# First diffusion step: column-scaled rows as a GpSimd product in place of their own transposes

## The chip, the cores and the metric

The kernel runs on one core of a Trainium2 chip. The metric is the time of one execution in microseconds on the device, the median of repeated runs. Engines are named as the profile names them: PE (TensorE matmul), PEld (its weight load), DVE (VectorE), ACT (ScalarE), POOL (GpSimd), SP (SyncE, which only issues DMAs). A name with q behind it (SPq, POOLq) is the engine's queue.

## What is computed

There are N = 2708 rows of D = 512 numbers. A graph attention layer comes first (layer 0). Then comes layer 1, a diffusion with three branches and two steps, here cut to what matters:

```
S  = adj + eye(N)
Rf = S / S.sum(axis=1)[:, None]      # each row divided by its row sum
Rb = S / S.sum(axis=0)[:, None]      # each row divided by the column sum of the same index
Xf = Xb = Xa = X
for s in range(2):
    A  = softmax of the nucleus (mass 0.9) of each row of the logits made from Xa
    Xf, Xb, Xa = Rf @ Xf, Rb @ Xb, A @ Xa
    Z += Xf @ U1[s] + Xb @ U2[s] + Xa @ U3[s]
out = x + layernorm(X + Z) * gamma + beta
```

In the first step `Xf` and `Xb` both start from X, so both are S @ X, with row i divided by a row sum in one and by a column sum in the other.

## The kernel before

The 2708 rows are 22 tiles of up to 128 rows (`NT`), handled in 11 pairs (`pairs`) and in 6 quads of two pairs (`quads`). Layer 0 runs to about 1095 us of the span, the first diffusion step to about 2300 us, and the second to the end. Inside a step the order on PE, ACT, DVE and SP is the order of the Python code (a manual schedule); POOL's order and that of layer 0 are left to a scheduler.

For each pair a step does the following.

- `Logits.products` (L521 on PE, L523 on ACT) makes the pair's logits `p`, `Logits.exp` looks at them on ACT (L553, L560), and `search` finds each row's nucleus on DVE: a few rounds of masses (L629), then `finish` (L806, L808, L730), then `branch`, which reads a flag into a DVE register and takes an arm of a switch (L890). `p` has four buffers, so the products of pair g + 2 wait until the search of pair g is through its branch.
- `attended` transposes the kept weights on PE (L1016, copied by ACT at L1020) and multiplies them with the values `va` (L1035). ACT takes the result out of PSUM with its scale (L1043) and POOL stores it as `xa_d` (L1045). The PSUM tiles `a` have two buffers.
- `part` makes S @ X for a quad. `product` (L967) runs between the other matmuls, half of the 22 row blocks in an even pair and half in the next, odd one. Then `scaled` runs for each of the quad's tiles and each of the two scales: ACT scales out of PSUM into `xe` (L977, `rinv` or `cinv`), POOL stores that as `xfb_d` (L978), and `split_rows` splits it into two halves for the second step: two DVE instructions (L181, L182) and one store by POOL (L183, to `fhl_d` or `bhl_d`). The split has two buffers. So the odd pairs 1, 3, 5, 7 and 9 hold the splits, eight in a full quad; in DVE's queue they lie between the rounds and `finish` of the next pair's search.
- `diffused` loads the pair's rows of `xfb_d` back (L1001 on SP), both branches. `turned_rows` transposes them (L147 on PE, four 128x128 transposes a tile) and ACT copies the result out of PSUM into `v_t` (L149).
- `mixed` adds up the three products with U1, U2 and U3 in one PSUM tile per row tile (L1076), with the weight rows `u_k` loaded by SP (L1074). Before the matmuls of one branch are issued, the rows of the next branch are turned. The order is U1, U2, U3. In the last pair of the first step (`final`) it is U3, U1, U2. `project` (L160, L165 to L173) makes keys and queries for the second step, stored to `kq_d`.

Between layer 0 and the first step the sums are inverted: `rinv`, `cinv`, and `ratio`, which is the row sum over the column sum. The first step begins with four loads of `keys` (L930) and loads of the queries `q_t` (L509) on SP.

Of the kernel before, what the change touches and what calls it, by code (L numbers as in the profile page):

```python
# [9 lines left out]
F32 = mybir.dt.float32  # L10
# [5 lines left out]
OP = mybir.AluOpType  # L16
AX = mybir.AxisListType
PSUM = bass.MemoryType.PSUM
# [6 lines left out]
P = 128  # L25
# [28 lines left out]
def kernel(  # L54
# [19 lines left out]
    nc = tc.nc  # L74
# [5 lines left out]
    KD = D // P  # L80
    NT = -(-N // P)
    rows = [min(P, N - i * P) for i in range(NT)]
    cols = [slice(i * P, i * P + rows[i]) for i in range(NT)]
# [7 lines left out]
    G = 2  # L91
# [3 lines left out]
    dram = ctx.enter_context(tc.tile_pool(name="dram", bufs=1, space=DRAM))  # L95
# [17 lines left out]
    xfb_d = dram.tile([2, N, D], F32, name="xfb_d")  # L113
    xa_d = dram.tile([N, D], F32, name="xa_d")
    en_d = dram.tile([H, N], F32, name="en_d")
    rank_d = dram.tile([NT * P], BF16, name="rank_d")

    ident = const.tile([P, P], F32, name="ident")
# [6 lines left out]
    rinv = const.tile([P, NT], F32, name="rinv")  # L125
    cinv = const.tile([P, NT], F32, name="cinv")
    ratio = const.tile([P, NT], F32, name="ratio")

    def row_bcast(ap, n):
        return bass.AP(tensor=ap.tensor, offset=ap.offset, ap=[[0, P], [1, n]])  # L130
# [71 lines left out]
    with ExitStack() as l0:  # L202
# [13 lines left out]
        with tc.tile_pool(name="l0w", bufs=1) as wp, tc.tile_pool(name="l0p", bufs=2) as pp, \  # L216
# [13 lines left out]
            for k in range(KD):  # L230
                nc.sync.dma_start(
                    out=w_sb[:, k, :].rearrange("p (h d) -> p h d", h=H),
                    in_=w_gat[:, k * P:(k + 1) * P, :].rearrange("h p d -> p h d"),
# [27 lines left out]
            for t in range(NT):  # L261
                pr = rows[t]
                h = hts[t]
                pt = ps.tile([P, KD, P], F32, name="tp")
# [50 lines left out]
        small = l0.enter_context(tc.tile_pool(name="l0small", bufs=3))  # L315
# [82 lines left out]
        for ci, tiles in enumerate(tchunks):  # L398
# [4 lines left out]
            for t in range(NT):  # L403
                pr = rows[t]
# [16 lines left out]
            for grp, r_b in zip(hgroups, r_bs):  # L421
                po = [ps_o.tile([P, 512], F32, name="po")[:DV] for _ in grp]
                for t in range(NT):
                    pr = rows[t]
# [11 lines left out]
            final = ci == len(tchunks) - 1  # L436
# [17 lines left out]
    for r, c0, c1 in [(P, 0, NFULL), (rows[-1], NFULL, NT)]:  # L454
        if c0 == c1:
            continue
        s = (slice(0, r), slice(c0, c1))
        for v, inv in ((rsum, rinv), (csum, cinv)):
            nc.vector.tensor_scalar(v[s], v[s], 1.0, 1e-12, op0=OP.add, op1=OP.max)
            nc.vector.reciprocal(inv[s], v[s])  # L460
        nc.vector.tensor_mul(ratio[s], cinv[s], rsum[s])

# [449 lines left out]
    for s in range(STEPS):  # L914
        last = s == STEPS - 1
        with ExitStack() as st:
# [3 lines left out]
            up = st.enter_context(tc.tile_pool(name=f"s{s}u", bufs=4, reuse_waits="tile"))  # L920
            parts = None if last else st.enter_context(tc.tile_pool(name=f"s{s}parts", bufs=2, reuse_waits="tile"))
            small = st.enter_context(tc.tile_pool(name=f"s{s}small", bufs=2, reuse_waits="tile"))
# [20 lines left out]
            def part(half, b):  # L943

                if b // 2 >= len(quads):
                    return []
                quad = quads[b // 2]  # L950
                first = b % 2 == 0
                w = len(quad) * P
                hl_d = (fhl_d if first else bhl_d) if last else vhl_d
                cs = range(NT) if last else range(0, NT // 2) if first else range(NT // 2, NT)
                steps = []

                def product(c):
                    if c == 0:
                        half[:] = [ps_s.tile([P, D], F32, name=f"q{i}") for i in range(len(quad))]
                    hl = sp.tile([P, 2, D], F32R, name="hl", bufs=3)  # L960
                    nc.sync.dma_start(out=hl.bitcast(F32), in_=hl_d[c * P:(c + 1) * P])
                    s_r = sp.tile([P, 2 * G * P], F32R, name="s_r")
                    nc.sync.dma_start(out=s_r[:, :w].bitcast(F32),
                                      in_=s_d[c * P:(c + 1) * P, quad[0] * P:quad[0] * P + w])
                    for j in range(len(quad)):
                        for h in range(2):
                            nc.tensor.matmul(half[j], lhsT=s_r[:, j * P:(j + 1) * P], rhs=hl[:, h],  # L967
                                             start=(c == 0 and h == 0), stop=(c == NT - 1 and h == 1))

                def scaled(t, ps, i, inv, to):  # L970
                    pr = rows[t]

                    if last and b < 2 and t % 2:
                        x = work.tile([P, D], F32, name="xw", bufs=2)
                    else:
                        x = work.tile([P, D], F32, name="xe", bufs=2 if last else 4)
                    nc.scalar.activation(x[:pr], ps[:pr], AF.Copy, scale=inv[:pr, t:t + 1])  # L977
                    nc.gpsimd.dma_start(out=xfb_d[i, cols[t], :], in_=x[:pr])  # L978
                    if not last:
                        split_rows(parts, nc.vector, x[:pr], t, to)  # L980

                steps += [lambda c=c: product(c) for c in cs]
                if last or not first:
                    for j, t in enumerate(quad):
                        if first or not last:
                            steps.append(lambda j=j, t=t: scaled(t, half[j], 0, rinv, fhl_d))
                        if not first:
                            steps.append(lambda j=j, t=t: scaled(t, half[j], 1, cinv, bhl_d))
                return steps

            def paced(steps, n):
                for step in steps[:n]:
                    step()
                del steps[:n]

            def diffused(grp):
                out_ = []
                for i in range(2):
                    for t in grp:
                        x = work.tile([P, D], F32, name=f"x{i}")  # L1000
                        nc.sync.dma_start(out=x[:rows[t]], in_=xfb_d[i, cols[t], :])  # L1001
                        out_.append(x)
                return out_[:len(grp)], out_[len(grp):]

            def attended(grp, keep, rden, fills, others, then):

# [50 lines left out]
            def turned_rows(grp, v):  # L1057
                return [transposed(up, ps_t, v[i], rows[t], "v_t") for i, t in enumerate(grp)]

            def mixed(grp, v_t, xf, xb, xa, others, fills, final=False):  # L1060

                pz = [ps_a.tile([P, D], F32, name="a") for _ in grp]
                if final:

                    v_t = turned_rows(grp, xa)
                    for i, t in enumerate(grp):
                        project(small, ps_t.tile([P, 512], F32, name="t"), v_t[i], t, s + 1)
                for n, u in enumerate((u3, u1, u2) if final else (u1, u2, u3)):  # L1070
                    nxt = turned_rows(grp, ((xf, xb) if final else (xb, xa))[n]) if n < 2 else None
                    for k in range(KD):
                        u_k = up.tile([P, D], F32, name="u_k", bufs=4 if last else 3)
                        nc.sync.dma_start(out=u_k, in_=u[s, k * P:(k + 1) * P, :])  # L1074
                        for i, t in enumerate(grp):
                            nc.tensor.matmul(pz[i][:rows[t]], lhsT=v_t[i][:, k, :rows[t]], rhs=u_k,  # L1076
                                             start=(n == 0 and k == 0), stop=(n == 2 and k == KD - 1))
                        paced(others, 1)
                        if n < 2 and k < 3:
                            paced(fills, 1)  # L1080
                    if n == 2 and not last and not final:
                        for i, t in enumerate(grp):
                            project(small, ps_t.tile([P, 512], F32, name="t"), v_t[i], t, s + 1)
                    v_t = nxt
                out_ = []
                for i, t in enumerate(grp):
                    pr = rows[t]
                    y = work.tile([P, D], F32, name="yo")
                    nc.scalar.copy(y[:pr], pz[i][:pr])
                    z = work.tile([P, D], F32, name="xw", bufs=2) if last else va[:, t, :]  # L1090
                    if last:
                        nc.sync.dma_start(out=z[:pr], in_=y_d[cols[t], :])
                    nc.gpsimd.tensor_tensor(y[:pr], y[:pr], z[:pr], op=OP.add)  # L1093
                    if not last:
                        nc.gpsimd.dma_start(out=y_d[cols[t], :], in_=y[:pr])
                    out_.append((t, y))
                return out_
# [66 lines left out]
            with tc.manual_schedule(engines={PE, ACT, DVE, SP}):  # L1164
# [18 lines left out]
                for g in range(-1, NP):  # L1183
# [18 lines left out]
                    if g >= 0:  # L1202
                        others.insert(0 if g else len(others) // 3, lambda g=g: rows_in.extend(diffused(pairs[g])))
                        final = g == NP - 1 and not last
# [72 lines left out]
```

## Time and profile before

| | us |
|---|---|
| runs (three), median | 3711.15 |
| lowest and highest | 3710.86, 3714.24 |
| the profiled execution's own time | 3711.47 |
| its span in the profile | 3709.7 |
| mean granted TensorE clock | 0.963 |
| layer 0, until the first product of logits | 1095.3 |

The profile is of one execution. Its span runs from the first to the last instruction on the engines, so the execution's own time is 1.8 us longer. "Busy" is the time that an engine's instructions took. A view of waits says which engine's line waited for which line, with the total, the number of times and the longest. A timeline's rows have start, length, engine, line, operation, operands (out<-in, partitions x elements), the count of merged instructions, and in brackets the idle time before them with what ended it. One matmul of the source is two records on PE where it is done in two passes, as at L1076 and L1035.

### The profile page before, as it was taken

To read this page: it belongs to the slowest core of one execution; us is meant where nothing else is said; L and a number is where in the kernel's file an instruction comes from. 1 tells how busy PE (TensorE), PEld (TensorE's weight loads), DVE (VectorE), ACT (ScalarE), POOL (GpSimd) and SP (SyncE) were. 2 spreads that over 40 slices of the span, in tenths; PEclk is the share of its full clock that TensorE was granted. 3 is DMA by queue.
4 is the path that set the end of the run, shared out by engine and by line. 5 is a ranking of instruction groups with operands and counts; after the bars stand their busy time and mean duration, and the time that the engine had idled before them with its cause. 6 is when DMAs were issued, how large, how long until landed. Compare 5 with 4: busy or idle time off the path is not lost. (4 is left out here: it accounts for less than half of the span.)

```text
span 3709.7 us, 35331 instructions
## 1 busy us (share of the span) xinstructions
PE 3376.1 (91%) x11143; PEld 1757.7 (47%) x11143; DVE 2612.0 (70%) x4820; ACT 1541.7 (42%) x2334; POOL 808.4 (22%) x1119
## 2 busy tenths in 40 slices
PE   7998999998956898989899899678999999999898
PEld 4432333333434455545455453445555565556452
DVE  4587888989947537374454652958978779777991
ACT  2343212111124764555666612335654556445511
POOL 4114240514331121121211121301112112121101
PEclk9999999999978999999999999999999999999999
DMA  3476424233237454454545353855655666566652
GB/s 113 152 251 239 141 79 151 82 104 106 70 99 274 139 195 166 156 179 148 199 149 189 122 193 104 302 191 195 206 188 205 234 216 204 184 212 234 202 200 66
DMA packets 276458, 634.08 MB, mean 171 GB/s; under 512 B 37209, under 2 KB 70441, under 8 KB 273243
## 3 DMA queue, kind: packets, MB, share of 16 engines
q1 hardware_dynamic: 249183, 540.99, 44.4%
q0 software_dynamic: 27024, 90.30, 6.4%
q8 instruction: 89, 1.46, 0.2%
q14 instruction: 162, 1.33, 0.1%
HBM read 509.07 MB, written 122.10 MB: 170 GB/s over the span
## 5 line engine op out<-in xcount | busy, mean ns | idle before, releaser
L1035 PE MATMUL a<-va,at 128*128 128x512 f32 (+2 forms) x1936 | 895.6, 602 | 39.6 <-ACT at L1020 39.5
L967 PE MATMUL q<-hl,s_r 128*128 128x512 f32 x2904 | 824.5, 430 | 61.1 <-DMA s_r<-s_d 60.9
L429 PE MATMUL po<-e,fw 128*65 128x512 f32 (+4 forms) x2112 | 838.9, 552 | 32.9 <-DVE e L427 23.3
L427 DVE SCALAR_TENSOR_TENSOR e<-r_b,kk,a_c 128x512 f32<-128x512 f32 (+4 forms) x1056 | 751.1, 740 | 68.5 <-PE po L429 18.1
L967 PEld LDWEIGHTS q<-hl,s_r 128*128 128x128 f32 x2904 | 547.9, 191 | 306.3 <-issue 135.4
L553 ACT ACTIVATE junk_a<-p,nth 128x2708 uint8<-128x2708 f32 (+1 forms) x240 | 613.2, 2555 | 68.8 <-POOL nth L572 65.1
L429 PEld LDWEIGHTS po<-e,fw 128*65 128x65 f32 (+1 forms) x2112 | 285.9, 139 | 546.6 <-issue 270.8
L1035 PEld LDWEIGHTS a<-va,at 128*128 128x128 f32 (+2 forms) x1936 | 339.2, 188 | 408.5 <-issue 346.7
L1076 PE MATMUL a<-u_k,v_t 128*128 128x512 f32 (+1 forms) x1056 | 491.4, 603 | 19.6 <-ACT xa L1043 14.4
L629 DVE SCALAR_TENSOR_TENSOR junk<-p,th 128x2708 bf16<-128x2708 f32 (+1 forms) x132 | 401.3, 3040 | 4.0
L1020 ACT COPY at<-t 128x512 f32<-128x512 f32 (+3 forms) x308 | 140.4, 477 | 478.6 <-PE t L1016 478.4
L1076 PEld LDWEIGHTS a<-u_k,v_t 128*128 128x128 f32 (+1 forms) x1056 | 189.4, 187 | 240.6 <-issue 183.8
L521 PE MATMUL t<-keys,q_t 128*128 128x452 f32 x528 | 165.3, 439 | 94.7 <-ACT p L523 73.6
L181 DVE TENSOR_SCALAR split_hl<-xe 128x512 int32<-128x512 int32 (+1 forms) x44 | 19.1, 434 | 263.4 <-ACT xe L977 217.0
L808 DVE MAX8 vn<-keep 128x8 f32<-128x2708 f32 (+1 forms) x66 | 196.8, 2981 | 2.3
L523 ACT COPY p<-t 128x452 f32<-128x452 f32 (+2 forms) x264 | 132.2, 539 | 123.2 <-PE t L521 85.6
L411 ACT ACTIVATE s_c<-a_c 128x512 fp32r<-128x512 f32 (+3 forms) x132 | 76.2, 578 | 250.1 <-DMA a_c<-in_adj_t_dram 124.8
L1016 PE MATMUL t<-ident,keep 128*128 128x128 f32 (+1 forms) x968 | 147.4, 274 | 26.4 <-DVE keep L757 18.8
L521 PEld LDWEIGHTS t<-keys,q_t 128*128 128x128 f32 x528 | 90.1, 208 | 165.4 <-ACT p L523 126.4
L1016 PEld LDWEIGHTS t<-ident,keep 128*128 128x128 f32 (+1 forms) x968 | 115.0, 139 | 106.8 <-issue 78.6
L548 DVE TENSOR_REDUCE nmx<-p 128x1 f32<-128x2708 f32 (+1 forms) x44 | 129.1, 2966 | 43.4 <-ACT p L523 43.4
L565 POOL TENSOR_TENSOR x<-sums,powers 128x4 f32<-128x4 f32 x22 | 43.7, 1987 | 507.9 <-ACT p L560 481.9
(296 smaller groups left out, 3160.6 us busy)
## 6 DMA issues: line engine op xcount, KB each, us to landing
s_r<-s_d SPq DMA_DIRECT2D x330, 256.0 KB
hl<-vhl_d SPq DMA_DIRECT2D x132, 512.0 KB
u_k<-in_L_gnn_U_dram SPq DMA_DIRECT2D x264, 256.0 KB
hl<-fhl_d SPq DMA_DIRECT2D x132, 512.0 KB
hl<-bhl_d SPq DMA_DIRECT2D x132, 512.0 KB
arow<-in_adj_dram SPq DMA_DIRECT2D x21, 1354.0 KB
s_d<-s_c SPq DMA_DIRECT2D x88, 256.0 KB
a_c<-in_adj_t_dram SPq DMA_DIRECT2D x84, 256.0 KB
```

What stands on the lines that cost most here:

```text
L427: nc.vector.scalar_tensor_tensor(e[:pr, :cw], r_b[:pr, i, :cw], kk[:pr, t, hd:hd + 1], a_c[t][:pr, :cw], op0=OP.max, op1=OP.mult)
L429: nc.tensor.matmul(po[i][:, :cw], lhsT=fw[:pr, t, hd, :], rhs=e[:pr, :cw], start=(t == 0), stop=(t == NT - 1))
L521: nc.tensor.matmul(pl[:, :c1 - c0], lhsT=q[:, i], rhs=self.keys[:, c0:c1], start=(i == 0), stop=(i == 1))
L523: nc.scalar.copy(p[:pr, c0:c1], pl[:pr, :c1 - c0])
L553: nc.scalar.activation(junk[:pr], self.p[i][:pr], func, **kw)
L629: v.scalar_tensor_tensor(junk_b[:pr], ps_[i][:pr], th, ps_[i][:pr], op0=OP.is_ge, op1=OP.mult, accum_out=dst)
L808: v.max(vs, keep[0][:pr])
L967: nc.tensor.matmul(half[j], lhsT=s_r[:, j * P:(j + 1) * P], rhs=hl[:, h], start=(c == 0 and h == 0), stop=(c == NT - 1 and h == 1))
L1016: nc.tensor.transpose(pt[:rows[c], j, :pr], keep[i][:pr, cols[c]], ident[:pr, :pr])
L1020: nc.scalar.copy(at[:r, j0:j1, :pr], pt[:r, j0:j1, :pr])
L1035: nc.tensor.matmul(pa[:pr], lhsT=at[:rows[c], j, :pr], rhs=va[:rows[c], c, :], start=(c == 0), stop=(c == NT - 1))
L1076: nc.tensor.matmul(pz[i][:rows[t]], lhsT=v_t[i][:, k, :rows[t]], rhs=u_k, start=(n == 0 and k == 0), stop=(n == 2 and k == KD - 1))
```

## The change

In the first step alone, the rows scaled by column sums are no longer stored, loaded back and transposed for the product with U2. Their transposes are made on GpSimd from those of the row-scaled tiles. In the transposed layout each row of X is a column, so every column is multiplied by its ratio. For this the 22x128 ratios are written once to device memory as a row (`rat_d`), by way of a transpose on PE and a copy on ACT, and each pair loads its 256 ratios broadcast to all 128 partitions (`ratios`). The splits to `bhl_d` stay. The second step is left as it is.

```diff
+    rat_d = dram.tile([NT * P], F32, name="rat_d")
...
     ratio = const.tile([P, NT], F32, name="ratio")
+    nc.vector.memset(ratio, 0.0)
...
         nc.vector.tensor_mul(ratio[s], cinv[s], rsum[s])
+    with tc.tile_pool(name="rat", bufs=1) as pool, tc.tile_pool(name="rat_ps", bufs=1, space=PSUM) as ps:
+        pt = ps.tile([NT, P], F32, name="ratio_t")
+        nc.tensor.transpose(pt, ratio, ident)
+        ratio_t = pool.tile([NT, P], F32, name="ratio_t")
+        nc.scalar.copy(ratio_t, pt)
+        nc.sync.dma_start(out=rat_d.rearrange("(t p) -> t p", p=P), in_=ratio_t)
...
                     nc.scalar.activation(x[:pr], ps[:pr], AF.Copy, scale=inv[:pr, t:t + 1])
-                    nc.gpsimd.dma_start(out=xfb_d[i, cols[t], :], in_=x[:pr])
+                    if last or i == 0:
+                        nc.gpsimd.dma_start(out=xfb_d[i, cols[t], :], in_=x[:pr])
...
             def diffused(grp):
                 out_ = []
-                for i in range(2):
+                if not last:
+                    ratios = small.tile([P, G * P], F32, name="ratios")
+                    nc.sync.dma_start(out=ratios[:, :len(grp) * P],
+                                      in_=row_bcast(rat_d[grp[0] * P:(grp[-1] + 1) * P], len(grp) * P))
+                for i in range(2 if last else 1):
                     for t in grp:
                         x = work.tile([P, D], F32, name=f"x{i}")
                         nc.sync.dma_start(out=x[:rows[t]], in_=xfb_d[i, cols[t], :])
                         out_.append(x)
-                return out_[:len(grp)], out_[len(grp):]
+                return out_[:len(grp)], out_[len(grp):] if last else ratios
...
+            def times(grp, v_t, ratios):
+                out_ = []
+                for i, t in enumerate(grp):
+                    pr = rows[t]
+                    x = up.tile([P, KD, P], F32, name="v_t")
+                    nc.gpsimd.tensor_tensor(x[:, :, :pr], v_t[i][:, :, :pr],
+                                            ratios[:, i * P:i * P + pr].unsqueeze(1).to_broadcast([P, KD, pr]), op=OP.mult)
+                    out_.append(x)
+                return out_
...
                 for n, u in enumerate((u3, u1, u2) if final else (u1, u2, u3)):
-                    nxt = turned_rows(grp, ((xf, xb) if final else (xb, xa))[n]) if n < 2 else None
+                    if n == 2:
+                        nxt = None
+                    elif not last and n == final:
+                        nxt = times(grp, v_t, xb)
+                    else:
+                        nxt = turned_rows(grp, ((xf, xb) if final else (xb, xa))[n])
```

## The prediction

> **What bounds the kernel now.** The page first: TensorE is busy nine tenths of the span, GpSimd has room.
>
> ```profile
> span 3709.7 us, 35331 instructions
> PE 3376.1 (91%) x11143; PEld 1757.7 (47%) x11143; DVE 2612.0 (70%) x4820; ACT 1541.7 (42%) x2334; POOL 808.4 (22%) x1119
> ```
>
> An average hides who waits last, so I read TensorE's waits inside the first step (1210 to 2270 us; columns: total us, times, longest).
>
> ```profile
> PE t L521 <- ACT p L523: 40.8, 25, 11.0
> PE a L1035 <- ACT at L1020: 15.6, 12, 10.3
> PE a L1076 <- ACT xa L1043: 10.4, 5, 2.3
> ```
>
> Four idle stretches of 7.2 to 11.0 us at L521 hold 34.6 of the 40.8. They come once in two pairs, so I read the timeline of an odd pair (the second; columns: start, length, engine, line, op, operands, count, idle time and what ended it).
>
> ```profile
> 1372.31 0.43 DVE L181 TENSOR_SCALAR split_hl<-xe 128x512 int32<-128x512 int32 x1 [42.81 <-ACT xe L977]
> 1380.13 1.11 POOL L978 DMA_DIRECT2D xfb_d<-xe  x2 [1.18 <-ACT xe L977]
> 1380.32 1.04 ACT L149 COPY v_t<-t 128x512 f32<-128x512 f32 x2
> 1382.60 0.54 POOL L183 DMA_DIRECT2D bhl_d<-split_hl  x1 [1.35 <-DVE split_hl L182]
> 1385.61 0.50 DVE L181 TENSOR_SCALAR split_hl<-xe 128x512 int32<-128x512 int32 x1 [1.94 <-ACT xa L1043]
> 1387.13 0.54 POOL L183 DMA_DIRECT2D bhl_d<-split_hl  x1 [1.25 <-DVE split_hl L182]
> 1391.64 0.43 DVE L181 TENSOR_SCALAR split_hl<-xe 128x512 int32<-128x512 int32 x1 [3.38 <-DMA bhl_d<-split_hl]
> 1420.22 0.97 ACT L523 COPY p<-t 128x452 f32<-128x452 f32 x2 [7.43 <-DVEq L890]
> 1420.82 6.72 PE L521 MATMUL t<-keys,q_t 128*128 128x452 f32 x16 [8.26 <-ACT p L523]
> ```
>
> Here eight splits of diffused rows stand in VectorE's queue ahead of the nucleus search's finish. There are two buffers, so each split waits for the store two before it to land: split, issue on GpSimd, landing, split. The last at 1391.64 starts finish and branch, whose end at 1420.22 lets ScalarE refill `p`, and TensorE goes on. From 1372 on TensorE is off the path in an odd pair. In even pairs TensorE leads, but one place pins it:
>
> ```profile
> 1702.74 2.57 ACT L553 ACTIVATE junk_a<-p,nth 128x2708 uint8<-128x2708 f32 x1
> 1704.02 1.09 PE L147 MATMUL t<-ident,x 128*128 128x128 f32 x8
> 1704.95 3.49 PE L1076 MATMUL a<-u_k,v_t 128*128 128x512 f32 x7
> 1705.29 0.69 ACT L1043 ACTIVATE xa<-a,rden 128x512 f32<-128x512 f32 x1
> 1706.03 0.30 PEld L1076 LDWEIGHTS a<-u_k,v_t 128*128 128x128 f32 x2 [0.88 <-ACT xa L1043]
> ```
>
> The eight transposes at 1704.02 are the ones removed: 0.93 us until L1076 starts. The pair's second tile needs the PSUM bank that L1043 empties, and L1043 stands behind a 2.57 us activation. Last, the entry into the step:
>
> ```profile
> 1075.99 15.87 SPq L930 DMA_DIRECT2D keys<-kq_d  x4
> 1095.30 8.81 PE L521 MATMUL t<-keys,q_t 128*128 128x452 f32 x24 [19.06 <-DMA q_t<-kq_d]
> ```
>
> **What the skill says.** The Trainium skill, "SBUF — State Buffer", section "SBUF: two separate sides": GpSimd and a VectorE op with two SBUF inputs lock one port pair against each other for whole instructions. The trace agrees: L572 on POOL takes 3.11 us beside VectorE's L629 of 3.04, and 0.25 elsewhere. "Perfetto Trace Analysis", "Tensor Engine Instruction": ScalarE, VectorE and GpSimd are strict FIFO; L1043 above agrees. "DMA: Bandwidth & Descriptors", "Anatomy of one DMA — SWDGE (gpsimd) path": about 2.0 us plus bytes/436e3, an estimate of 3.2 us for a 512 KB split store; the trace has medians of 3.2 (`fhl_d`) and 3.5 (`bhl_d`), least 2.9.
>
> **The change, part by part.**
>
> *Transposes gone (22 tiles, 88 transposes).* 8 cost 0.93 us, so 11 pairs hold 10.2 us. What counts: in the even pairs 0, 2, 4, 6 the second tile's loads would start at 1704.84 + 2 x 0.43 = 1705.70 but for L1043 and do at 1706.03; the gain ends at 0.33 each, 1.3 in all. Pair 8 already waits 1.09 us for L1043: nothing. Odd pairs 1, 3, 5, 7: nothing (each waits 2.34 for L1043, and over 7 at L521). Pair 9 has no products to wait for and L1043 ends as L1076 starts: 0.9. The last pair then waits 0.45 and 0.53 us for `u_k`; its loads move ahead of three `q_t` loads on SP: 0 to 1.9, taken 0.5. Sum -2.7 (-4.1 to -1.3).
>
> *ScalarE copies gone:* 11 x 1.04 us after L1043. In odd pairs the last split waits for a landing, not for `xe`; in even ones VectorE has the next odd pair's 42.81 us of slack. Nothing; without that cover they gain up to 11 us.
>
> *DMAs.* 22 stores of 256 KB leave POOL's queue (0.54 us each), 22 loads leave SP's; 11 loads of `ratios` enter SP's ahead of `hl` and `s_r`, which are wanted 10 us later: nothing.
>
> *The products on GpSimd.* No row has this shape with this broadcast. L367, two inputs and one broadcast, takes 1.03 to 1.48 us; L1093 1.29; L374 up to 1.71. Taken 1.3, two per pair 2.6. Used after the eight `u1` matmuls, 6.9 us on, so TensorE waits only if a product is blocked for over 4 us: nothing (0 to 3 us in a pair). In even pairs only `xa_d` is queued behind. **In odd pairs the order of the built program puts both products ahead of the fourth split's `bhl_d` store.** They start when the first `v_t` copy ends, about 1381.1, and hold POOL until 1383.8: that store goes from 1382.60 to 1383.8, so the sixth split, which waits for it, from 1385.61 to 1386.8, and its store from 1387.13 to about 1388.1. Against it, two `xfb_d` stores before each landing are gone. This last store took 4.4 us to land (issue 1387.13, split 1391.64); at the 3.5 median the last split starts at 1391.7. So +0.1 us. Ends: with a 2.9 us landing -0.6; with products of 1.7 us beside VectorE and no relief +2. Taken +0.3 x 4 pairs = +1.2 (-2.4 to +8).
>
> *The ratio row.* Its memset, transpose, copy and 11 KB store run once. The transpose waits for the PSUM banks of layer 0, so for ScalarE's last L166 there, which ends at 1085.9; the store issues at about 1087 and stands on SP ahead of `keys`, whose first two loads (1.31 MB) left at 1076. They now share 1087 to 1095 with the last `kq_d` stores and the `q_t` loads. At the page's highest slice, 302 GB/s, they take 4.3 us and are done in time; at its mean of 171, 7.7, to 1095. Cost 0 to 4, taken +2, all on the path.
>
> *Sum:* -2.7 + 1.2 + 2.0 = +0.5 us on the profiled execution's 3711.47 (span 3709.7, 1.8 around it), 0.3 above the median of 3711.15. On the median: 3711.6, rounded to **3711.5 us**.
>
> **Rivals.**
> - *Cancelled* (above): 3705 with every term at its lower end (-4.1 - 2.4 = -6.5 us), 3718.7 with the last pair's gain gone, 1.2 us per odd pair and 4 at the entry. For it: L1043 and L890 end the waits. 0.64.
> - *TensorE counts after all, or the splits speed up:* all 10.2 us, 3701; or 1 us less per odd chain from the lighter store queue with the -2.7, 3704. For it: 91% busy, landings of 4.4 us where 2.9 is possible. Against: L1043 is not moved. 0.19.
> - *The products block the split stores:* VectorE's splits and the products take the port in turns, the fourth split's store goes 2.5 us later, and the last split with it: 4 x 2.5 + 2, less 2.7: 3720.5. It decides from about 1.2 us, where the lost backlog no longer makes up for it; slower by 7.4 us needs 2 us a pair. 0.17.
>
> That the products would not replace the transposes is excluded: the built program has neither the transposes nor the copies.
>
> **From this to the numbers.** A measurement of this kernel can tell about 0.2%, 7.4 us, from no change. Faster 0.19, same 0.64, slower 0.17. The range 3700 to 3720 reaches from the full gain to the blocked stores and leaves out a tenth at each end.
>
> **What would show it.** Right: a wait for L1043 of about 1 us in even pairs where 0.3 was; the last split of odd pairs within 1 us of where it stood from the first; L521 still idle 7 to 11 us; `keys` issued near 1087, first L521 at 1096 to 1099. Wrong: even pairs 0.9 us shorter; L521's idle grown by over 2 us; products over 2 us or L1076 waiting for POOL.

## The result and the profile after

The changed kernel is slower: **3741.1 us** (median of four, 3738.5 to 3745.6) against 3712.7 for the kernel before, run beside it. The ratio is 1.008, 95% interval 1.0066 to 1.0093. The prediction said 3711.5, within 3700 to 3720. Its profiled execution took 3743.29 us. From the page:

```profile
span 3741.2 us, 35148 instructions
...
PE 3375.9 (90%) x11056; PEld 1752.4 (47%) x11056; DVE 2629.1 (70%) x4821; ACT 1530.9 (41%) x2313; POOL 844.9 (23%) x1119
```

POOL is 36 us busier: the 22 products add 28, the 22 stores that are gone take off 11, and the rest are other instructions of GpSimd's that take longer than before. Line numbers have moved: L521, L523 are now L530, L532; L1076 is L1107; L1043 is L1059; L181 to L183 are L184 to L186; L885 is L894; L890 is L899; L1093 is L1124; the products are L1081. TensorE's waits inside the first step:

```profile
PE t L530 <- ACT p L532: 57.8, 31, 13.2
PE a L1107 <- ACT xa L1059: 18.1, 9, 3.2
```

The first row was 40.8 and is 57.8. Most of it is the wait for the branch in the odd pairs, so here is the timeline of the second pair (pair 1):

```profile
1374.23 0.43 DVE L184 TENSOR_SCALAR split_hl<-xe 128x512 int32<-128x512 int32 x1 [42.83 <-ACT xe L986]
...
1382.80 0.43 DVE L184 TENSOR_SCALAR split_hl<-xe 128x512 int32<-128x512 int32 x1 [2.75 <-ACT v_t L152]
1383.26 3.16 DVE L185 TENSOR_TENSOR split_hl<-xe,split_hl 128x512 f32<-128x512 f32 x1
1383.36 2.50 POOL L1081 TENSOR_TENSOR v_t<-v_t,ratios 128x512 f32<-128x512 f32 x2
...
1386.72 0.60 POOL L186 DMA_DIRECT2D bhl_d<-split_hl  x1 [0.86 <-DVE split_hl L185]
...
1391.31 0.54 POOL L186 DMA_DIRECT2D bhl_d<-split_hl  x1 [1.91 <-DVE split_hl L185]
...
1396.73 0.43 DVE L184 TENSOR_SCALAR split_hl<-xe 128x512 int32<-128x512 int32 x1 [4.30 <-DMA bhl_d<-split_hl]
...
1427.52 1.88 PE L530 MATMUL t<-keys,q_t 128*128 128x452 f32 x4 [12.97 <-ACT p L532]
```

The fourth split's subtraction takes 3.16 us where all others take 0.69: it stands beside both products and is through 0.56 us after they end (1385.86). In pairs 3 and 7 it is the same; in pair 5 the split's first instruction meets the products and takes 2.00 in place of 0.43. Its store leaves 12.49 us after the first split, where it left after 10.29. The last split is 22.5 us after the first, and was 19.3. TensorE's idle is 12.97 us and was 8.26. From the last split to VectorE's last instruction ahead of the branch it is 28.7 us, where it was 27.1: one 0.15 us instruction of the branch, shown in before and in after, now falls beside POOL's second L1124.

```profile
1418.52 0.15 DVE L885 SCALAR_TENSOR_TENSOR flag_t<-flag_t,weights 1x3 f32<-1x3 f32 x1
```

```profile
1423.54 1.84 DVE L894 SCALAR_TENSOR_TENSOR flag_t<-flag_t,weights 1x3 f32<-1x3 f32 x1
1423.95 1.41 POOL L1124 TENSOR_TENSOR yo<-yo,va 128x512 f32<-128x512 f32 x1
```

The even pair looks as the prediction said: the transposes are gone, and the second tile waits 0.88 us for L1059, behind an activation of 2.56.

```profile
1714.13 2.56 ACT L562 ACTIVATE junk_a<-p,nth 128x2708 uint8<-128x2708 f32 x1
...
1715.41 1.12 PE L1107 MATMUL a<-u_k,v_t 128*128 128x512 f32 x2
...
1716.68 0.69 ACT L1059 ACTIVATE xa<-a,rden 128x512 f32<-128x512 f32 x1
...
1717.42 4.56 PE L1107 MATMUL a<-u_k,v_t 128*128 128x512 f32 x10 [0.88 <-ACT xa L1059]
```

And the entry, where `keys` are issued behind the row of ratios (1081.84):

```profile
1084.56 2.60 SPq L939 DMA_DIRECT2D keys<-kq_d  x4
...
1094.79 6.62 PE L530 MATMUL t<-keys,q_t 128*128 128x452 f32 x16 [13.31 <-DMA q_t<-kq_d]
```

To see where the time goes, I compare the first copy of `p` in each pair (its "mark") with the kernel before. The second column is another execution of the changed kernel, taken later, against the same trace of before.

| loss in | us | again |
|---|---|---|
| up to the mark at 1309 (entry, first pair) | +1.9 | +4.0 |
| pairs 1, 3, 5, 7 | +4.8 +4.8 +2.9 +6.1 = 18.5 | +4.2 +4.8 +3.3 +6.3 = 18.6 |
| pairs 2, 4, 6 | +1.6 | +1.6 |
| from there to the last store | +3.3 | +3.2 |
| behind the last store | +6.1 | +6.1 |
| sum; spans differ by | 31.5; 31.5 | 33.5; 33.4 |

The last row can be read from the two timelines' last stores, of before and of after:

```profile
3705.88 0.53 POOL L1109 DMA_DIRECT2D out_dram<-yo  x1 [0.76 <-DVE yo L1108]
```

```profile
3731.28 0.54 POOL L1140 DMA_DIRECT2D out_dram<-yo  x1 [0.76 <-DVE yo L1139]
```

From there to the span's end it is 3.8 us in before and 9.9 in after. Nearly all of it is one DRAIN of GpSimd, 3.02 and 9.14 us long (durations in ns, least/median/longest; before, then after). The tables call it the last wait.

```profile
L1272 POOLq DRAIN  x3: 40/107/3018, 3705.9 to 3709.4; - x3
```

```profile
L1303 POOLq DRAIN  x3: 40/107/9144, 3731.2 to 3740.9; - x3
```

It is not the landing of the last store: in both kernels that has landed 1.8 us after its issue.

### The profile page after: what moved, and what is told of

It is laid out like the page before. It is cut to its first block, busy times and chain, and to the rows that moved or that the text cites. A ratio compares the mean times of both kernels' runs of the same rounds, so it can differ in the third digit from the quotient of the medians.

```text
span 3741.2 us, 35148 instructions
## 1 busy us (share of the span) xinstructions
PE 3375.9 (90%) x11056; PEld 1752.4 (47%) x11056; DVE 2629.1 (70%) x4821; ACT 1530.9 (41%) x2313; POOL 844.9 (23%) x1119
## 3 DMA queue, kind: packets, MB, share of 16 engines
q0 software_dynamic: 25312, 84.76, 5.9%
## 5 line engine op out<-in xcount | busy, mean ns | idle before, releaser
L432 PE MATMUL po<-e,fw 128*65 128x512 f32 (+4 forms) x2112 | 840.2, 553 | 34.6 <-DVE e L430 23.0
L1107 PE MATMUL a<-u_k,v_t 128*128 128x512 f32 (+1 forms) x1056 | 499.3, 610 | 25.6 <-ACT xa L1059 22.2
L1107 PEld LDWEIGHTS a<-u_k,v_t 128*128 128x128 f32 (+1 forms) x1056 | 191.0, 189 | 260.0 <-issue 196.5
L530 PE MATMUL t<-keys,q_t 128*128 128x452 f32 x528 | 165.0, 440 | 106.7 <-ACT p L532 92.2
L184 DVE TENSOR_SCALAR split_hl<-xe 128x512 int32<-128x512 int32 (+1 forms) x44 | 20.3, 460 | 269.0 <-ACT xe L986 218.8
L532 ACT COPY p<-t 128x452 f32<-128x452 f32 (+2 forms) x264 | 131.3, 539 | 140.9 <-PE t L530 87.5
L530 PEld LDWEIGHTS t<-keys,q_t 128*128 128x128 f32 x528 | 90.8, 209 | 176.7 <-ACT p L532 142.4
L1032 PE MATMUL t<-ident,keep 128*128 128x128 f32 (+1 forms) x968 | 147.1, 274 | 26.6 <-DVE keep L766 18.8
```

What stands on the lines that cost most here:

```text
L432: nc.tensor.matmul(po[i][:, :cw], lhsT=fw[:pr, t, hd, :], rhs=e[:pr, :cw], start=(t == 0), stop=(t == NT - 1))
L530: nc.tensor.matmul(pl[:, :c1 - c0], lhsT=q[:, i], rhs=self.keys[:, c0:c1], start=(i == 0), stop=(i == 1))
L532: nc.scalar.copy(p[:pr, c0:c1], pl[:pr, :c1 - c0])
L1032: nc.tensor.transpose(pt[:rows[c], j, :pr], keep[i][:pr, cols[c]], ident[:pr, :pr])
```

## The experiments

Theory 1: in odd pairs the products stand in GpSimd's queue, and on the port it shares with VectorE, ahead of the fourth split's store; the chain of split, store and landing starts the rest late. Theory 2: what all pairs share is to blame (the row, its loads, fewer transposes and less traffic). Times and ratios are of repeated runs. The next three columns are from the traces, means over pairs 1, 3, 5 and 7, in us; before and after are means of two traces each there.

| kernel | time | ratio to before | 4th store after 1st split | last split after 1st | last split to branch | last wait |
|---|---|---|---|---|---|---|
| before | 3709 to 3713 | | 10.2 | 19.1 | 27.5 | 3.02 |
| after | 3741.1 | 1.0080 | 12.6 | 22.4 | 28.7 | 9.14 |
| even | 3718.1 | 1.0019 (1.0012 to 1.0027) | 10.6 | 19.6 | 27.9 | 2.49 |
| odd | 3719.6 | 1.0023 (1.0014 to 1.0031) | 11.0 | 19.9 | 28.8 | 2.56 |
| vec | 3716.5 | 1.0017 (1.0009 to 1.0024) | 10.2 | 19.8 | 28.3 | 9.14 |
| nolock | 3741.2 | 1.0083 (1.0069 to 1.0097) | 11.8 | 21.0 | 27.9 | 9.14 |
| late_dep | 3721.6 | 1.0026 (1.0019 to 1.0032) | 10.2 | 19.6 | 26.3 | 9.14 |
| parts3 | 3697.8 | 0.9963 (0.9950 to 0.9977) | 9.1 | 15.3 | 25.4 | 9.14 |
| vec_parts3 | 3693.6 | 0.9951 (0.9938 to 0.9965) | 9.2 | 15.5 | 25.3 | 9.14 |
| vp3_stores | 3685.2 | 0.9933 (0.9919 to 0.9947) | 9.0 | 15.5 | 25.2 | 3.01 |
| vp3_tiny | 3696.0 | 0.9961 (0.9946 to 0.9976) | 9.1 | 15.5 | 25.0 | 9.47 |

**Products in even pairs only, and in odd pairs only** (even, odd). The other pairs store, load and transpose as before; one buffer for the ratios makes the room. This line is of even; odd has `== 1`.

```diff
-                    elif not last and n == final:
+                    elif not last and n == final and (grp[0] // 2) % 2 == 0:
```

> The products stand in the even pairs alone; the odd pairs store, load and transpose the column-scaled rows as before. Theory 1 (the products delay the split stores of the odd pairs): the trace of the changed kernel puts 18.6 us of the loss into the odd pairs 1, 3, 5 and 7, 1.3 at the entry and 2.3 into the even pairs 0, 2, 4 and 6. So this kernel loses 3 to 4 us: 3714 to 3716 us, idle at L521 in odd pairs back at 7 to 11 us. Theory 2 (what all pairs share, the row of ratios, its loads on SP, the lighter traffic, is to blame): about half of the loss stays, 3724 to 3727.

> The products stand in the odd pairs alone. Theory 1: the four odd pairs keep their 18.6 us and the entry its 1.3: 3730 to 3732 us, the fourth split's subtraction at 3.2 us beside the products, the idle at L521 at 12 to 13 us. Theory 2: half of the loss, 3724 to 3727. If the two halves do not add up to the whole (about 25 us), something depends on both.

Measured 3718.1 and 3719.6. The first is 2 us above what theory 1 gave, and neither theory had the second: by the ratios the halves lose 7 and 9 us, together 16 of some 30. The reason lies in the built order. In the odd-pairs kernel the scheduler puts the products behind the seventh split's store, not ahead of the fourth's; no subtraction is stretched, and pairs 1, 3 and 5 lose 1.6, 2.5 and 0.2 us. So the place in the queue was moved by accident, and had to be moved on purpose. In both kernels pair 7 loses 5.1 us, in one of them with no product in it; the section on the hardware comes back to that.

**Products behind the splits' stores** (late_dep). This is the experiment that decides. The call moves behind the U1 matmuls, and in odd pairs one edge orders the products behind the eighth split's store. In the first step as built, the products of pairs 1, 3, 5 and 7 are all that has moved.

```diff
-                        nxt = times(grp, v_t, xb)
+                        nxt = None
...
+                        with tc.issue_after(stored[0].ins):
+                            v_t = times(grp, v_t, xb)
```

> As the changed kernel, with one thing moved: in odd pairs both products are queued on GpSimd behind the eighth split's store, where they stood ahead of the fourth's. All other instructions and their order are the same. Theory 1 (place in GpSimd's queue): the last split comes back to 19.3 us after the first, from 22.3; of the 4.65 us that each odd pair loses, 3 to 4.65 come back: 3722 to 3729 us against the changed kernel's 3741. Rival (TensorE): the products now end some 5 us after TensorE has finished with U1, so it waits; the idle of 8 us at L521's place should cover this, and if it does not, the gain is given back and the time stays at 3736 to 3741. Theory 2 (row, loads, traffic): 3741, the order does not matter.

Measured 3721.6: 20 of the 30 us come back. Its second pair (L186 to L188 are the split here, L532, L1109 and L1083 the lines L530, L1107 and L1081 above):

```profile
1383.27 0.69 DVE L187 TENSOR_TENSOR split_hl<-xe,split_hl 128x512 f32<-128x512 f32 x1
...
1384.25 0.53 POOL L188 DMA_DIRECT2D bhl_d<-split_hl  x1 [0.90 <-DVE split_hl L187]
...
1392.75 0.43 DVE L186 TENSOR_SCALAR split_hl<-xe 128x512 int32<-128x512 int32 x1 [2.87 <-DMA bhl_d<-split_hl]
...
1394.75 4.46 POOL L1083 TENSOR_TENSOR v_t<-v_t,ratios 128x512 f32<-128x512 f32 x2
```

The subtraction is back at 0.69 and the last split 18.5 us after the first (19.6 in the mean of the four pairs). Against the trace of before, the four pairs lose -0.7, -0.8, -2.4 and +1.6 us. The products now come too late for TensorE, and the waits show that this costs nothing:

```profile
PE t L532 <- ACT p L534: 23.2, 25, 6.4
...
PE a L1109 <- POOL v_t L1083: 9.9, 4, 3.1
```

TensorE waits 9.9 us for products that were never waited for before, and its wait for `p` shrinks from 57.8 to 23.2. Its last store is 1.5 us later than before's, and the last wait adds 6.1: 7.6 us in its trace.

**Products on VectorE** (vec).

```diff
-                    nc.gpsimd.tensor_tensor(x[:, :, :pr], v_t[i][:, :, :pr],
+                    nc.vector.tensor_tensor(x[:, :, :pr], v_t[i][:, :, :pr],
```

> The products run on VectorE in place of GpSimd, all else as changed. In an odd pair they stand in VectorE's queue after the seventh split, where it waited 3.4 us for a landing; in an even pair ahead of the search's finish. Theory 1: nothing holds GpSimd's queue or the shared port, so the last split of an odd pair stands again about 19.3 us after the first and the loss of 18.6 us goes: 3711 to 3716 us. Theory 2: the row, the loads and the lighter traffic are still there, so the loss stays, 3733 to 3737. A third outcome: VectorE's wait for the transposes delays the eighth split or the finish by 1.4 us or more in each pair: 3717 to 3725.

Measured 3716.5, half a microsecond above what theory 1 gave. The product takes 0.69 us on VectorE where it took 1.27 on GpSimd, and the fourth store leaves as before. The row, the loads and the lighter traffic are all still there, so theory 2 falls for 25 of the 30 us. The 6 that stay are about as much as the last wait, which is 6.1 us longer here too.

**A subtraction that reads one tensor of SBUF** (nolock; `src` is the tile in PSUM), to tell the queue (1a) from the port (1b).

```diff
-        eng.tensor_tensor(hl[:pr, 1], x, hl[:pr, 0], op=OP.subtract)
+        if src is None:
+            eng.tensor_tensor(hl[:pr, 1], x, hl[:pr, 0], op=OP.subtract)
+        else:
+            eng.scalar_tensor_tensor(hl[:pr, 1], src, inv, hl[:pr, 0], op0=OP.mult, op1=OP.subtract)
```

> As the changed kernel, but the subtraction of a split takes its first operand scaled from PSUM, so that it reads one tensor of SBUF and not two. Theory 1a (GpSimd's queue: the fourth split's store stands behind both products): the subtraction is back at about 0.7 us where it took 3.2, yet its store cannot leave before the products end; 0.7 us of the 3.2 in each of the pairs 1, 3 and 7 come back: 2 to 3 us, to about 3735 against the changed kernel's 3737 without its long last wait. Theory 1b (the port: the stretched subtraction is what delays the store): 2.5 us in each of these pairs, some 7.5 in all: about 3729.

The time says nothing, 3741.2: this kernel loses 14 us more than the changed one up to the mark at 1309. 12 of them are one wait of TensorE for `p`, 26.6 us where it is 14.2; why, I did not follow up. The odd pairs can be read by themselves. Beside the products (1397.44 to 1399.94) the subtraction is not stretched, but the next split's first instruction is:

```profile
1397.27 0.75 DVE L188 SCALAR_TENSOR_TENSOR split_hl<-q,cinv,split_hl 128x512 f32<-128x512 f32 x1
...
1398.31 1.92 DVE L184 TENSOR_SCALAR split_hl<-xe 128x512 int32<-128x512 int32 x1 [0.28 <-DMA fhl_d<-split_hl]
```

Of the 2.3 us that the fourth store came late, 0.8 go, and of the 3.3 us of the last split 1.4. The next split still meets the products, so this kernel is the queue with a part of the port. By it the queue is at most some 60% of the loss in the splits, and the port at least some 40%: an estimate, since this run left that meeting in place. Its four odd pairs lose 10.0 us where the changed kernel lost 18.5; the 8.5 that come back are nearer to what 1b gave (7.5) than to 1a (2 to 3).

**Three buffers for the splits** (parts3), with and without the products on VectorE (vec_parts3). The rows that are no longer loaded had held 4 KB a partition, which is what the third buffer takes. In parts3 the scheduler also moves the products, to behind the fifth split's store; vec and vec_parts3 have none on GpSimd and differ in the buffers alone.

```diff
-            parts = None if last else st.enter_context(tc.tile_pool(name=f"s{s}parts", bufs=2, reuse_waits="tile"))
+            parts = None if last else st.enter_context(tc.tile_pool(name=f"s{s}parts", bufs=3, reuse_waits="tile"))
-                    ratios = small.tile([P, G * P], F32, name="ratios")
+                    ratios = small.tile([P, G * P], F32, name="ratios", bufs=1)
```

> As the changed kernel, with three buffers for the splits in place of two and one for the ratios in place of two, which makes the room. A split waits for the landing of the store three before it. The built order moves too: the products stand behind the sixth split's fhl store. Theory 1 (the chain split, store, landing is what the odd pairs wait for): the last split follows its xe, about 16 us after the first in place of 22.3; 5 to 7 us less in each of four odd pairs: 3713 to 3721 us. If something else holds the odd pairs (search, TensorE), the last split moves and the idle of TensorE does not: 3735 to 3741.

> Products on VectorE and three buffers for the splits. If the two causes are separate, the kernel with the products on VectorE (3716.5 us, 6.4 above before) gains 3 us in each of four odd pairs, since the last split no longer waits 3.4 us for a landing: about 3704 to 3707 us, under both kernels. If the products on VectorE, which wait for TensorE's transposes and ScalarE's copies ahead of the eighth split, are now what it waits for, 3710 to 3717.

Measured 3697.8 and 3693.6, both under the kernel before and better than I expected. From vec to vec_parts3 the buffers alone are worth 23 us. With the products on GpSimd, TensorE's wait for `p` in the first step is 16.3 us, in all of it:

```profile
PE t L530 <- ACT p L532: 16.3, 36, 2.2
```

So the chain of splits is what the odd pairs waited for. That it was so before the change too fits, since each odd pair is now 4.9 to 6.3 us shorter than in before; before itself with a third buffer was not run. On VectorE the products fit between the seventh and the eighth split, and what was an idle of 8.26 us is 3.08:

```profile
1384.12 1.28 DVE L1081 TENSOR_TENSOR v_t<-v_t,ratios 128x512 f32<-128x512 f32 x2
...
1412.59 0.74 PE L530 MATMUL t<-keys,q_t 128*128 128x452 f32 x1 [3.08 <-ACT p L532]
```

**Second traces of both kernels** (before_again, after_again), with nothing changed.

> The kernel before, for a second trace: how much the marks of the pairs (first copy of p in each pair, last split, GpSimd's last wait) move between two executions of one program. Theory 1 wants the odd pairs of before to stay within 2 us of the first trace, so that the 2.9 to 6.1 us of the changed kernel are its own; the last wait of GpSimd, 3.0 us in before and 9.1 in the changed one, is taken to vary by itself if it differs here.

> The changed kernel, for a second trace. If the loss has its cause in the order of GpSimd's queue, the four odd pairs lose again 2.9 to 6.1 us each against both traces of before, the fourth split's subtraction takes again about 3.2 us in most of them, and GpSimd's last wait is 9.1 us. If these were accidents of one execution, they differ.

3711.7 and 3745.2 us. Pairs 1, 3, 5 and 7 of before move by 0.0, +2.6, -1.7 and +0.4, one of them more than expected, but those of after repeat to 0.6 us, with subtractions of 3.15 us in the same three pairs. The last wait is again 3.02 and 9.14: it belongs to the program, and my guess that it varies by itself was wrong.

**The last wait** (vp3_stores, vp3_tiny): vec_parts3, once with the stores of the column-scaled rows put back, which nobody reads, and once with 11 small stores.

```diff
-                    if last or i == 0:
+                    if True:
                         nc.gpsimd.dma_start(out=xfb_d[i, cols[t], :], in_=x[:pr])
```

```diff
             def times(grp, v_t, ratios):
+                nc.gpsimd.dma_start(out=spare_d[grp[0]:grp[0] + 1], in_=ratios[:1, :16])
```

> Products on VectorE and three buffers for the splits (3693.6 us), with the 22 stores of column-scaled rows put back, which nobody reads. GpSimd's last instruction waits 3.02 us in both traces of the kernel before (308 DMAs issued by GpSimd), 2.5 us with 296 and 298, and 9.14 us in all six kernels with 286. If it goes by GpSimd's DMAs, it is back at 3.0 us and 6.1 us come off the end; against that the stores take 0.54 us each of GpSimd's queue and stand among the split stores, 1 to 2 us in each of four odd pairs: 3689 to 3696 us. If the wait does not go by them, it stays at 9.1 us: 3695 to 3701.

> Products on VectorE and three buffers for the splits, with 11 stores of 64 bytes added on GpSimd, one a pair of the first step, away from the split stores: 297 DMAs in all. If the last wait goes by the count of GpSimd's DMAs, it is about 2.5 us and the time 3687 to 3690 us. If it goes by their packets or bytes, it stays at 9.1 us: 3693 to 3696.

With the dead stores the wait is 3.01 us and the kernel the fastest of all, 3685.2, below its forecast: its last store is 1.1 us later than in vec_parts3, and 6.1 come off the end. With the small stores it stays, 9.47, with 297 DMAs on GpSimd; even has 296, and 2.49. So it does not go by the number of DMAs, but by what they move. GpSimd's queue has 27024 packets in the first and 25664 in the second (25312 without them). Whether packets or bytes count, these runs do not tell.

## Why the prediction was wrong

- **The place of the bound was right.** The odd pairs are bound by the chain of splits and not by TensorE: late_dep makes TensorE wait 9.9 us more and is faster than the changed kernel, and the third buffer shortens the pairs.
- **The transposes** gained nothing that can be seen: pairs 2, 4 and 6 lose 1.6 us in place of gaining 1.0, and those of before_again vary by up to 1.2 each. L1059 pins the second tile as said (0.88 us waited). (The upper end of 3718.7 for "cancelled" leaves out pair 9's 0.9 us as well as the last pair's 0.5; nothing hangs on it.)
- **The products' own time was right:** 1.28 and 1.27 us on GpSimd, 1.3 taken.
- **The step that failed is "+0.3 x 4 pairs"** for the products ahead of the fourth store. The prediction let the store wait for the end of the products alone (1.2 us) and gave that back by a faster landing. Measured per odd pair: the store leaves 2.3 us later, since the split in front of it is itself stretched beside the products (from 0.69 to 3.16 in three of the four pairs). The last split is 3.3 us later. The landing of the sixth store is not faster: 4.5 us on average in the two traces of after and 4.3 in those of before. And the branch is another 1.2 us later (28.7 in place of 27.5), as the finish, once late, meets POOL's additions. The 3.3 and the 1.2 make the 4.6 us that the pairs lose each, 18.5 in all, against 1.2 in the sum. This is 17 of the 31 us by which the profiled execution missed it. One of the prediction's own signs of being wrong came with it: the four long idles at L521 grew from 34.6 us to 50.5.
- **The rival "the products block the split stores" is what happened**, through the place that it named and the port. Its 2.5 us a pair hold for the store; 0.8 us more of the last split and the finish were missing. It had a chance of 0.17. The port was written down under the skill and then left out of the likeliest case's sum. The Trainium skill, "SBUF — State Buffer", section "Who interferes with whom", says that a VectorE instruction with two SBUF inputs contends with a GpSimd instruction that reads SBUF, that the pair of ports they share is an exclusive lock, and that the order of issue decides which of the two blocks. The 3.16 us agree with a lock, though the subtraction shows the earlier start here, by 0.1 us; and in late_dep it is the other way round: the first product takes 3.23 us beside VectorE's keep of 3.03, and the second 1.26.
- **The ratio row** (+2): `keys` left at 1084.56 and not at 1087, and the first L530 came 0.5 us earlier than in before, 2.5 later in the second trace, while before itself moves by 1.9. The cost is within that, 0 to 4 as said.
- **Not in the sum at all:** the last wait, 6.1 us. The prediction took the 22 stores that leave GpSimd's queue as free or a gain.
- **Open:** some 3 us in the second step, from its second to its third first copy of `p` (2392 to 2491): 98.9 and 99.3 us in the two traces of after, 95.9 and 94.9 in those of before, at most 97.7 in the other kernels. The granted clock in the 30 us from 2420 is 0.94, and 1.00 in the same stretch of before and of late_dep. No run tells why.

## What to carry to other kernels

Before work is moved to an idle engine, write down its queue at that place, and follow whoever waits for what then stands behind it; an engine that is 22% busy can carry a chain that sets the end. Where a split, a store and a landing follow each other through two buffers, try a third one first: here it took 23 us off the kernel with the products on VectorE and brought it under the kernel before, which no change to the links alone did. Where a trace shows instructions of two engines longer side by side than apart, price both sides of the meeting, and the instruction behind each.

## What the hardware showed that I had not expected

GpSimd pauses now and then ahead of a DMA, with nothing in the profile that it waits for ("issue"). The timelines of GpSimd show it in before, in after and in the even-pairs kernel (one row of each):

```profile
1943.83 0.74 POOL L173 DMA_DIRECT2D kq_d<-kq_hl  x1 [2.62 <-issue]
```

```profile
2039.75 0.54 POOL L186 DMA_DIRECT2D bhl_d<-split_hl  x1 [4.21 <-issue]
```

```profile
2012.84 0.55 POOL L988 DMA_DIRECT2D xfb_d<-xe  x1 [4.75 <-issue]
```

Counted along GpSimd's queue, these are pauses ahead of the 191st DMA in before and of the 190th in the other two. Each idle is some 2.3 us longer than is usual at its place (0.29 ahead of L173 and 1.91 ahead of L186, for instance). Others, idles of 2.0 and 3.3 us, stand ahead of the 96th in after and of the 290th in the even-pairs kernel.

In before the pause falls ahead of a store of keys for the second step. In the changed and the even-pairs kernel it falls among the splits of pair 7, where one store is about 2 us later than in the other odd pairs. This fits that pair 7 loses most in the changed kernel, and 5.1 us in the even-pairs kernel, where its own work was not changed. With the dead stores put back (vp3_stores) the pause is again ahead of the 191st DMA, a store of keys, and no store of pair 7 is late.

The changed kernel issues 286 DMAs and has 9.14 us of last wait. A third such pause may fall on the end of the kernels with 25312 to 25664 packets, and lie earlier, under other work, in those with 26112 and more: in the even-pairs kernel it comes after 25648. Two things speak against a simple count. The last wait is longer by 6.1 us and not by 2.3, and the second pause comes after 17472 packets in before, 17648 in after and 17392 in the even-pairs kernel. What GpSimd does in a pause, and what sets the distance, was not tried.
